# Conditioned attention on one Trainium2 core: the last two GpSimd operations moved to VectorE

## The chip, the core and the metric

The kernel runs on one core of a Trainium2 chip. A core has five engines that run their own instruction streams and meet only at semaphores: TensorE (PE, matrix products, its weight loads shown as PEld), VectorE (DVE), ScalarE (ACT), GpSimd (POOL) and SyncE (SP, which here only issues transfers). Sixteen DMA engines move data between the device memory and the on-chip memories, SBUF (128 partitions) and PSUM (128 partitions in 8 banks, where TensorE writes). The metric is the device time of one execution in microseconds (us).

## What is computed

The inputs are x, 8 batches of 512 rows of 512 features, one conditioning vector of 512 features for each batch, and the weights and biases of one attention layer with 16 heads of 32 features. All is in 32-bit floating point.

```python
Q = _split_heads(x @ Wq.T + bq)
K = _split_heads(x @ Wk.T + bk)
V = _split_heads(x @ Wv.T + bv)
tQ = _split_heads(tokens @ Wq.T + bq)
tK = _split_heads(tokens @ Wk.T + bk)
cQ = Q + tQ
cK = K + tK
scores = jnp.einsum('bhqd,bhkd->bhqk', cQ, cK) / jnp.sqrt(jnp.float32(HEAD_DIM))
attn = jax.nn.softmax(scores, axis=-1)
out = jnp.einsum('bhqk,bhkd->bhqd', attn, V)
...
x = x + _L0_cond_ref(x, cond_1024[:, None, :], ...)
```

So for each query row of each head: weights exp(score - maximum), their sum as the denominator, the weighted sum of the value rows divided by it, and x added.

## The kernel before

**Tiles.** A tile is one batch and a group of four heads (128 features), so there are T = 8 x 4 = 32 tiles, 0 to 31. A tile's scores are 4 heads of 512 x 512. TensorE makes the scores, VectorE takes row maxima, ScalarE exponentials, and TensorE multiplies the exponentials with the value rows (`times_v`). The main loop runs over tiles 1 to 28 and mixes the steps of neighbouring tiles; tiles 29, 30 and 31 are written out by hand behind it, and all that this change touches is in that last part, where `t = T - 1` (tile 31) and `t - 1` is tile 30.

**What sets the order.** The order on TensorE, ScalarE, VectorE and GpSimd is the order in which the program text issues the operations (`manual_schedule`). A framework adds the semaphores. An engine works through its queue in order, so an instruction that waits holds everything behind it. A transfer is issued by the queue that it names: `nc.sync` is SyncE's, `nc.scalar` ScalarE's.

**Tile 30's output.** For the earlier tiles, `send` (line 809) transposes the product with V on VectorE into the layout of the output (32 x 32 blocks), multiplies by the reciprocal denominators on GpSimd (line 813) and adds x there (line 814). Tile 29 goes that way (`send_parts`), and its line 814 is the last GpSimd operation ahead of the two that are moved. For tile 30 the same steps are written out: the denominators come from a product with ones of the summed exponentials (`times_ones(acc, pd, ...)`, line 755), are transposed (line 1267) and inverted (line 1270); the product with V is transposed into `y30` (line 1272); GpSimd multiplies `y30` by the reciprocals (line 1274) and adds `x30`, which is x with the bias of the values in it (line 1275). `store_30` (line 1277) sends one 32-partition quarter of `y30` at a time to the output: quarters 0 and 1 by SyncE (line 1282), 2 by ScalarE (line 1294), 3 by ScalarE as the very last transfer of the program (line 1325). All four are issued at line 1280.

**Tile 31's end.** While this happens TensorE makes tile 31's last exponentials' scores, denominators (line 755) and product with V (line 745). Then:

- VectorE multiplies the denominators with x into `part_x` (line 1291), and ScalarE copies the denominators (line 1293).
- In two halves VectorE adds `part_x` to the product with V (line 1302) and TensorE transposes the sum back (line 1304). Between the halves TensorE transposes the copied denominators (`untranspose`, line 836).
- VectorE inverts the denominators (line 1309) and multiplies each half by them (line 1314), so that (product + denominator x x) / denominator = attention + x.
- Four stores follow (line 1321), two each by ScalarE and SyncE, and quarter 3 of tile 30.

At the end of the program (line 1352 in the profile) each engine drains and then all engines meet.

Of the kernel before, what the change touches and what calls it, by code (L numbers as in the profile page):

```python
# [12 lines left out]
ALU = mybir.AluOpType  # L13
# [4 lines left out]
def kernel(  # L18
# [38 lines left out]
    nc = tc.nc  # L57
    P = 128
# [93 lines left out]
    BL = 32  # L152
    NB = S // BL

    def spread(a, d, n=1):

        return a.rearrange("(f j) d -> j f d", j=BL)[:, :, d : d + n * BL]
# [557 lines left out]
    def exponentials(t, kc, at=None):  # L715

        bank = [bank_of(i) for i in at] if at else [banks(i) for i in range(HG)]
        for j in range(HG):
            r = slice(j * HD, j * HD + 3)
            nc.tensor.matmul(bank[j], onesb[r, :], maxT[t][r, :], start=True, stop=False)  # L720
        for j in range(HG):
            r = slice(j * HD, (j + 1) * HD)
            nc.tensor.matmul(  # L723
                bank[j],
                qkT["k", t][r, kc * P : (kc + 1) * P],
                qkT["q", t][r, :],
                start=False,
                stop=True,
            )
        for pr in range(NP):  # L730
            e = room_for_e(t, kc, pr)
            es[t, kc, pr] = e
            for i in range(2):
                nc.scalar.activation(e[:, i, :], bank[pr * 2 + i], AF.Exp)  # L734
# [99 lines left out]
    def untranspose(o, pt):  # L834
        for qc in range(NS):
            nc.tensor.transpose(  # L836
                pt[:, qc * P : (qc + 1) * P], o[:, qc * P : (qc + 1) * P], ident
            )
# [136 lines left out]
    def late_part(i):  # L975
        return late[0][:, i, :]
# [292 lines left out]
    rec = op.tile([P, NB, 1], F32, tag="recs", name=f"recs_{t - 1}")  # L1269
    nc.vector.reciprocal(rec, den[:, :, 0:1])  # L1270
    y30 = late_part(13).rearrange("p (f e) -> p f e", e=BL)
    nc.vector.transpose(y30.rearrange("p f e -> p (f e)"), parts[t - 1])
    x30 = xr.pop(t - 1)
    nc.gpsimd.tensor_tensor(y30, y30, rec.broadcast_to([P, NB, BL]), ALU.mult)
    nc.gpsimd.tensor_tensor(y30, y30, x30, ALU.add)

    def store_30(queue, hs):
        b, g = divmod(t - 1, G)
        for h in hs:
            queue.dma_start(spread(out[b], h * P + g * BL), y30[h * BL : (h + 1) * BL])  # L1280

    store_30(nc.sync, (0, 1))
    exponentials(t, 3, (4, 2, 0, 1))
    times_v(t, 2, pv)
    pd = bank(7)
# [5 lines left out]
    nc.vector.tensor_tensor(part_x, pd, xr[t], ALU.mult)  # L1291
    den = late_part(11)
    nc.scalar.copy(den, pd)
    store_30(nc.scalar, (2,))
    oT = late[0][:, 0, :]
    y = late[0][:, 1, :].rearrange("p (c s) -> p c s", c=NS)
    rec = op.tile([P, NS, HG, 1], F32, tag="rec", name="rec")
# [3 lines left out]
    for i in range(2):  # L1301
        nc.vector.tensor_tensor(oT[:, two[i]], pv[:, two[i]], part_x[:, two[i]], ALU.add)  # L1302
        for qc in (i * 2, i * 2 + 1):
            nc.tensor.transpose(  # L1304
                po[i][:, qc * P : (qc + 1) * P], oT[:, qc * P : (qc + 1) * P], ident
            )
        if i == 0:
            untranspose(den, pi)
    nc.vector.reciprocal(  # L1309
        rec, pi.rearrange("p (c h e) -> p c h e", c=NS, h=HG)[:, :, :, 0:1]  # L1310
    )
# [45 lines left out]
```

## Time and profile before

| | |
|---|---|
| median of 3 runs | 681.99 us (680.9 to 684.14) |
| profiled execution, whole | 682.65 us |
| profiled execution, span | 680.4 us |
| TensorE busy | 660.6 us (97%) |
| VectorE busy | 578.9 us (85%) |
| ScalarE busy | 544.6 us (80%) |
| GpSimd busy | 340.7 us (50%) |

The profile is of one execution, so its own time and span stand beside the median. A row of a group of instructions reads: line, engine, operation, what it writes <- what it reads, shapes, count | busy us, mean ns of one | idle time of the engine before them and what ended it. A row of the timeline reads: start, duration, engine, line, operation, and in brackets the engine's idle time before it and what released it; neighbours of one kind are merged, so that "x2" is two instructions from the first one's start to the last one's end. An engine's name with q (POOLq, SPq) means its sequencer: drains, semaphores and the issue of transfers, which don't count as busy.

### The profile page before, as it was taken

To read this page: it belongs to the slowest core of one execution; us is meant where nothing else is said; L and a number is where in the kernel's file an instruction comes from. 1 tells how busy PE (TensorE), PEld (TensorE's weight loads), DVE (VectorE), ACT (ScalarE), POOL (GpSimd) and SP (SyncE) were. 2 spreads that over 40 slices of the span, in tenths; PEclk is the share of its full clock that TensorE was granted. 3 is DMA by queue.
4 is the path that set the end of the run, shared out by engine and by line. 5 is a ranking of instruction groups with operands and counts; after the bars stand their busy time and mean duration, and the time that the engine had idled before them with its cause. 6 is when DMAs were issued, how large, how long until landed. Compare 5 with 4: busy or idle time off the path is not lost. (4 is left out here: it accounts for less than half of the span.)

```text
span 680.4 us, 22874 instructions
## 1 busy us (share of the span) xinstructions
PE 660.6 (97%) x9100; PEld 312.6 (46%) x9100; DVE 578.9 (85%) x821; ACT 544.6 (80%) x1397; POOL 340.7 (50%) x449
## 2 busy tenths in 40 slices
PE   7989999999999999999999999999999999999993
PEld 6444454544544444444544444454544544454421
DVE  5897988989899898979889897898989898897793
ACT  1568788988979898898889888788988989897771
POOL 5551563565446464466635664464644666352531
PEclk9999999999999999999999999999999999999997
DMA  9718439386574938658383865729376573822011
GB/s 203 129 29 206 126 68 224 69 200 152 128 190 85 223 79 209 142 133 208 71 223 70 211 139 134 188 67 237 80 201 151 132 178 66 220 47 56 16 18 32
DMA packets 140814, 90.85 MB, mean 134 GB/s; under 512 B 117436, under 2 KB 126308, under 8 KB 140708
## 3 DMA queue, kind: packets, MB, share of 16 engines
q1 hardware_dynamic: 132196, 73.78, 47.5%
q0 software_dynamic: 5568, 14.95, 8.7%
q8 instruction: 72, 1.18, 0.8%
q10 hardware_dynamic: 2944, 0.66, 0.5%
q14 instruction: 34, 0.28, 0.1%
HBM read 20.27 MB, written 8.39 MB: 42 GB/s over the span
## 5 line engine op out<-in xcount | busy, mean ns | idle before, releaser
L664 ACT ACTIVATE psum<-psum,nmax 128x512 f32<-128x512 f32 x256 | 169.0, 663 | 52.5 <-DVE nmax L584 40.1
L584 DVE TENSOR_REDUCE nmax<-psum 128x1 f32<-128x512 f32 x270 | 171.4, 680 | 46.0 <-PE psum L617 45.5
L734 ACT ACTIVATE arena<-psum 128x512 f32<-128x512 f32 x264 | 136.9, 602 | 33.8 <-PE psum L723 24.4
L617 PE MATMUL psum<-kT,qT 32*128 32x512 f32 x1024 | 157.5, 621 | 1.4 <-ACT psum L664 1.4
L664 ACT ACTIVATE arena<-psum,nmax 128x512 f32<-128x512 f32 x224 | 152.6, 697 | 5.3 <-issue 4.2
L626 DVE TENSOR_REDUCE nmax<-psum 128x2 f32<-128x1024 f32 x115 | 139.3, 1212 | 1.1 <-PE psum L617 1.1
L637 DVE STREAM_TRANSPOSE blocks<-blocks 128x1024 f32<-128x1024 f32 x112 | 132.2, 1218 | 0.3 <-DMA blocks<-arena 0.2
L648 POOL DMA_DIRECT2D blocks<-arena x112 | 56.1, 506 | 78.8 <-ACT arena L664 69.2
L813 POOL TENSOR_TENSOR res<-res,recs 128x512 f32<-128x512 f32 x30 | 31.5, 1049 | 120.9 <-DVE res L812 120.9
L617 PEld LDWEIGHTS psum<-kT,qT 32*128 32x128 f32 x1024 | 59.5, 182 | 64.9 <-issue 24.0
L745 PE MATMUL psum<-arena,v 128*32 128x512 f32 x576 | 69.4, 597 | 0.0
L723 PE MATMUL psum<-qT,kT 32*128 32x512 f32 x528 | 68.5, 589 | 0.0
L745 PE MATMUL psum<-blocks,v 128*32 128x256 f32 x896 | 52.1, 381 | 0.0
L459 PE MATMUL psum<-wc_v,xc 128*32 128x256 f32 x768 | 50.6, 381 | 1.4 <-ACT v L497 1.4
L664 ACT ACTIVATION_READ_ACCUMULATOR psum<-psum,nmax 128x1 f32 x256 | 51.9, 203 | 0.0
L664 ACT ACTIVATION_READ_ACCUMULATOR arena<-psum,nmax 128x1 f32 x224 | 47.8, 213 | 0.0
L459 PE MATMUL psum<-xc,wc_q 128*32 128x256 f32 x720 | 47.4, 381 | 0.0
L459 PE MATMUL psum<-xc,wc_k 128*32 128x256 f32 x720 | 47.4, 381 | 0.0
L812 DVE STREAM_TRANSPOSE res<-psum 128x512 f32<-128x512 f32 x28 | 20.1, 717 | 23.3 <-PE psum L745 23.3
L814 POOL TENSOR_TENSOR xr<-res,xr 128x512 f32<-128x512 f32 x30 | 38.5, 1282 | 2.4
L207 POOL TENSOR_TENSOR xr<-xr,wT_q 128x512 f32<-128x512 f32 x30 | 38.4, 1279 | 0.2
L745 PEld LDWEIGHTS psum<-blocks,v 128*32 128x32 f32 x896 | 26.4, 110 | 25.0 <-ACT arena L734 10.6
(184 smaller groups left out, 934.4 us busy)
## 6 DMA issues: line engine op xcount, KB each, us to landing
blocks<-arena SPq DMA_DIRECT2D x336, 128.0 KB, 3.8
blocks<-arena POOLq DMA_DIRECT2D x112, 128.0 KB, 3.9
xr<-in_x_dram SPq DMA_DIRECT2D x60, 128.0 KB, 2.6
x<-in_x_dram SPq DMA_DIRECT2D x56, 128.0 KB, 3.5
out_dram<-xr SPq DMA_DIRECT2D x56, 128.0 KB, 2.4
w_q<-in_L_cond_Wq_dram SPq DMA_DIRECT2D x4, 256.0 KB, 4.4
w_k<-in_L_cond_Wk_dram SPq DMA_DIRECT2D x4, 256.0 KB
w_v<-in_L_cond_Wv_dram SPq DMA_DIRECT2D x4, 256.0 KB, 8.3
```

Of the source, the lines that this page charges most:

```text
L207: nc.gpsimd.tensor_tensor(xr[t], xr[t], bias, ALU.add)
L459: nc.tensor.matmul(pt[r], still[:, r], moving, start=(kc == kcs[0]), stop=(kc == kcs[-1]))
L584: nc.vector.tensor_reduce(nmax[t][:, qc, j : j + 1, 0], pt, AX.X, ALU.max, negate=True)
L617: nc.tensor.matmul(pt, qkT["q", t][r, qc * P : (qc + 1) * P], qkT["k", t][r, :], start=True, stop=True,)
L626: nc.vector.tensor_reduce(nmax[t][:, qc, pr * 2 : pr * 2 + 2, 0], pt, AX.X, ALU.max, negate=True)
L637: nc.vector.transpose(e, e)
L648: queue.dma_start(to.rearrange("p c h s -> p (c h s)"), of)
L664: nc.scalar.activation(to, of, AF.Exp, bias=nmax[t][:, qc, j, :], accum_out=sums[t][:, qc, j, :],)
L723: nc.tensor.matmul(bank[j], qkT["k", t][r, kc * P : (kc + 1) * P], qkT["q", t][r, :], start=False, stop=True,)
L734: nc.scalar.activation(e[:, i, :], bank[pr * 2 + i], AF.Exp)
L745: nc.tensor.matmul(pt[j * HD : (j + 1) * HD, at], vs[b % 2][:, kc, (g * HG + j) * HD : (g * HG + j + 1) * HD], e, start=(kc == chunks[0]), ...
L814: nc.gpsimd.tensor_tensor(xr[t], y, xr[t], ALU.add)
```

## The change

The multiplication and the addition that make tile 30's output are issued on VectorE instead of GpSimd. The multiplication keeps its place in the text, behind the transpose of line 1272. The addition moves down, behind both halves of tile 31's additions (line 1302) and ahead of its reciprocal (line 1309). The stores of quarters 0, 1 and 2 move with it, and are issued behind the addition; quarter 3 stays the last transfer. GpSimd has no operation behind tile 29's line 814.

```diff
     x30 = xr.pop(t - 1)
-    nc.gpsimd.tensor_tensor(y30, y30, rec.broadcast_to([P, NB, BL]), ALU.mult)
-    nc.gpsimd.tensor_tensor(y30, y30, x30, ALU.add)
+    nc.vector.tensor_tensor(y30, y30, rec.broadcast_to([P, NB, BL]), ALU.mult)
 
     def store_30(queue, hs):
...
-    store_30(nc.sync, (0, 1))
     exponentials(t, 3, (4, 2, 0, 1))
     times_v(t, 2, pv)
     pd = bank(7)
...
     den = late_part(11)
     nc.scalar.copy(den, pd)
-    store_30(nc.scalar, (2,))
...
         if i == 0:
             untranspose(den, pi)
+    nc.vector.tensor_tensor(y30, y30, x30, ALU.add)
+    store_30(nc.sync, (0, 1))
+    store_30(nc.scalar, (2,))
     nc.vector.reciprocal(
```

## The prediction

> **What bounds the kernel now.** I began with the end of the chain of waits, because the edit touches only the last stage. Columns: start, duration (both us), what.
>
> ```profile
> 667.89 0.88 PE psum L745 x6
> 668.77 0.02 issue
> 668.80 0.43 DVE late L1302
> ...
> 669.72 0.45 PE psum L836 x4
> 670.17 0.02 issue
> 670.19 0.27 DVE rec L1309
> ...
> 670.70 0.61 DVEq L1352
> ```
>
> The chain ends at 671.3, and the page's span is 680.4: 9.1 us of the program hold no compute on it. So the second view is the rows of line 1352, where the program ends (`q` marks an engine's sequencer; min/median/max duration in ns, then first and last start), first whole and then for 674.82 to 679.6 alone:
>
> ```profile
> span 680.4 us, 22874 instructions
> L1352 POOLq DRAIN  x3: 46/102/11037, 668.6 to 680.1; - x3
> L1352 SPq DRAIN  x3: 7/7/7, 674.8 to 679.9; - x3
> L1352 ACTq DRAIN  x2: 8/79/150, 673.1 to 679.9; - x2
> ```
>
> ```profile
> L1352 POOLq DRAIN  x1: 11037/11037/11037, 668.6 to 668.6; - x1
> L1352 SPq DRAIN  x1: 7/7/7, 674.8 to 674.8; - x1
> ```
>
> Each engine drains, and then all meet. ScalarE has drained at 673.2, SyncE (which waits for the stores) at 674.8. GpSimd's drain starts at 668.6 and takes 11.04 us, to 679.6, and in the 4.8 us before its end nothing else is recorded. From 679.6 to the span's end are 0.8 us of meeting. The waits of SyncE and the transfers of 676 to 681 agree:
>
> ```profile
> SPq L1352 <- PEq L1352: 5.5, 2, 5.0
> DMA packets 0, 0.00 MB, mean 0 GB/s; under 512 B 0, under 2 KB 0, under 8 KB 0
> ```
>
> The releaser named there is only the last engine to be let go; what ends at 679.6 is GpSimd's drain. So **the end is set by GpSimd**, not by tile 31's arithmetic. Is that length owed to the last GpSimd work? The start of the program has the only other drain of GpSimd outside the meeting, and it follows four tiny fills:
>
> ```profile
> L1343 POOLq DRAIN  x1: 183/183/183, 0.3 to 0.3; - x1
> ```
>
> A drain is thus not 11 us by nature; this one lasts until 9.7 us after GpSimd's last operation (table below: 668.62 + 1.27 = 669.89). One instance can't say what those 9.7 us are counted from. I read them as GpSimd's own, counted from its last work, because the drain starts as soon as its sequencer is through, while no other engine has finished.
>
> The stage itself, in order of time:
>
> ```profile
> 651.96 1.27 POOL L814 TENSOR_TENSOR xr<-res,xr 128x512 f32<-128x512 f32 x1
> 667.49 1.05 POOL L1274 TENSOR_TENSOR late<-late,recs 128x512 f32<-128x512 f32 x1 [14.26 <-DVE late L1272]
> ```
>
> ```profile
> 666.76 0.65 DVE L1272 STREAM_TRANSPOSE late<-parts 128x512 f32<-128x512 f32 x1
> ...
> 667.97 0.69 DVE L1291 TENSOR_TENSOR late<-psum,xT 128x512 f32<-128x512 f32 x1 [0.55 <-PE psum L755]
> 668.62 1.27 POOL L1275 TENSOR_TENSOR late<-late 128x512 f32<-128x512 f32 x1
> 668.69 0.59 ACT L1293 COPY late<-psum 128x512 f32<-128x512 f32 x1 [2.42 <-DVE late L1291]
> 668.80 0.76 DVE L1302 TENSOR_TENSOR late<-psum,late 128x256 f32<-128x256 f32 x2
> ...
> 669.55 0.60 PE L836 MATMUL psum<-ident,late 128*128 128x128 f32 x4
> ...
> 669.92 0.85 SPq L1280 DMA_DIRECT2D out_dram<-late  x2
> 669.92 0.38 ACTq L1280 DMA_DIRECT2D out_dram<-late  x1
> ...
> 670.19 0.26 DVE L1309 RECIPROCAL rec<-psum 128x16 f32<-128x16 f32 x1 [0.63 <-PE psum L836]
> 670.55 0.76 DVE L1314 TENSOR_TENSOR late<-psum,rec 128x256 f32<-128x256 f32 x2
> 671.00 1.60 SPq L1321 DMA_DIRECT2D out_dram<-late  x2
> 671.01 1.32 ACTq L1321 DMA_DIRECT2D out_dram<-late  x2
> 672.37 0.65 ACTq L1280 DMA_DIRECT2D out_dram<-late  x1
> ```
>
> **The change, part by part.** *Removed from GpSimd*: 1.05 us (L1274) and 1.27 us (L1275). Its last operation becomes L814, which ends at 653.23, as nothing of GpSimd lies between. The drain then starts at about 652 and ends at 653.23 + 9.7 = 662.9. What hides it is the work of tile 31 and its stores, to 674.8: a cover of 11.9 us. Without that cover it would cost 4.8 us, as now. The end is next set by SyncE: 674.8 + 0.8 = 675.6, so the ceiling of the gain is 680.4 - 675.6 = **4.8 us**, before what VectorE's new work takes off.
>
> *Added to VectorE*: two elementwise operations on 128x512 with both operands in SBUF. The nearest rows:
>
> ```profile
> L386 DVE TENSOR_TENSOR xc<-xc,xT 128x512 f32<-128x512 f32 x1 | 0.7, 692 | 0.1
> L1302 DVE TENSOR_TENSOR late<-psum,late 128x256 f32<-128x256 f32 x2 | 0.8, 420 | 0.1
> L1314 DVE TENSOR_TENSOR late<-psum,rec 128x256 f32<-128x256 f32 x2 | 0.8, 420 | 0.1
> ```
>
> So 0.69 us each; the broadcast factor costs nothing (420 ns at L1314, with one, and at L1302, without).
>
> *The multiplication* follows the transpose L1272, which ends at 667.41, and runs to about 668.13. It fills the 0.55 us in which VectorE waited for TensorE, and L1291 starts 0.08 to 0.17 us late. (Independent neighbours overlap by 0.08 us: the L1302 pair takes 0.76 us, not 2 x 0.42.) L1291 then ends at 668.74 to 668.82. Two wait for it. L1302 waits also for the product with V, which ends at 668.77, and so comes 0.0 to 0.1 us late; I take 0.06. ScalarE's copy of the denominators would end near 669.4, and the transposes that read it start at 669.55: covered, by some 0.15 us, and beyond that it would delay L1309.
>
> *The addition* stands between L1302, which ends at 669.56, and the reciprocal L1309. There VectorE waited 0.63 us for L836; the addition takes 0.69, less 0.08 of overlap at one side. That is 0 to 0.06 us more. Its operands are old by then (the multiplication, and x with its bias), so it waits for nothing; queued behind it are L1309, the pair L1314 and through them the four stores of L1321. Together I take **0.1 us** late at L1314. The ends for these two steps are 0 (both fit the gaps) and 1.38 us (neither does, 2 x 0.69).
>
> *Moved stores*: three of tile 30's four are released by the addition near 670.25 instead of by GpSimd at 669.89, some 0.35 us later. On SyncE the two take 0.85 us, to 671.1, which puts its part of L1321 back by 0.1 to 0.15 us, to an end near 672.75. On ScalarE one takes 0.38 us and is through by 670.7, before L1314 has anything ready. ScalarE's last store (672.37 + 0.65 = 673.02 now) stays the last issue, and moves by the 0.1. In the transfers of 671.3 to 673 (tenths busy of the DMA engines, slices of 0.0425 us) there is a hole from about 671.9 to 672.3:
>
> ```profile
> DMA  9999999999987631000000016999999999999996
> ```
>
> Before the hole are tile 30's three stores, behind it the other five. A delay of 0.35 us slides the three into the hole of 0.4 and pushes nothing; if it were 0.2 longer, the last landing would move by 0.1 to 0.2.
>
> *Sum*: -4.8 + 0.1 = -4.7 us: span 675.7. The profiled execution took 682.65 us, 2.25 more than its span, and would be 677.95; it stands 0.66 above the median of the runs, 681.99, against which the forecast is **677.3 us** (-0.69%).
>
> **Rivals.**
>
> *The drain belongs to the program's end, not to GpSimd's work.* Then it ends some 4.8 us behind the last landing whoever works last, and only the 0.1 us stays: 682.1. For it: one instance, and a long drain was seen only at the end. Against it: it starts at 668.6, 6 us before SyncE is through, and GpSimd's later drains in the meeting take 46 and 102 ns. [...]
>
> *Slower: the early drain holds up VectorE.* While GpSimd worked on L814, a VectorE cast took six times that of its like, and ended with it at 653.28:
>
> ```profile
> 652.07 1.21 DVE L678 CAST split<-nmax 128x16 bf16<-128x16 f32 x1
> ...
> 653.54 0.20 DVE L680 CAST split<-rest 128x16 bf16<-128x16 f32 x1
> ...
> 654.91 1.22 DVE L1147 TENSOR_TENSOR acc<-arena 128x1024 f32<-128x1024 f32 x1
> ```
>
> If the drain did the same, it would lie from 653.2 to 662.9 beside tile 30's and 31's sums, which read SBUF twice and keep VectorE without a gap (stretch, its length, then busy us of PE, PEld, DVE: 6.00 of 6.00):
>
> ```profile
> 660.00:666.00 6.00, 5.98 (x55) 1.47 (x51) 6.00 (x7) 4.84 (x11) 0.00 (x0) 1.00 0.00 0
> ```
>
> The sums would start 8.0 us late; the 0.55 of idle before L1291 gives some back, and -4.7 + 8.0 - 0.5 = +2.8: 684.8. It decides from a hold of about 5.2 us on. Against it: after 669.9 the present drain ran beside L1309 and L1314, which took their usual 0.26 and 0.42 us. [...]
>
> *Both operations in the open.* If the semaphores between them and their neighbours cost enough that neither fits its gap, 1.4 us of the 4.8 are given back: 678.6.
>
> **How the numbers follow.** Forecast 0.80, drain of the end 0.12, both in the open 0.05, held VectorE 0.03. For the range: gains from 4.8 (nothing late) down to 3.4 (both in the open), each against the runs of before, 680.9 to 684.14: 676.1 to 680.7. It leaves out the two rivals at 682.1 and 684.8, 0.15 together, and takes 0.1 more below. No change is what lies within 0.5%, 3.4 us here, about what a measurement of this kernel can tell apart: the forecast is beyond it with 0.92, the exposed case with half, the other two lie within or a little above. Faster 0.77, same 0.19, slower 0.04.
>
> **What would show it.** Right: GpSimd's long drain starts near 652 and ends before 665; SyncE's second drain stands at 674.9 to 675.1 and the span ends 0.8 behind it; L1309 starts at 670.2 to 670.35; tile 30's stores are issued at 670.2 to 670.35. Wrong: the long drain still ends some 5 us after SyncE's (first rival); L1147 and L1149 behind 654 last longer than 1.22 us or start late (second); L1314 starts after 671.5 (third).

## The result and the profile after

| | before | after |
|---|---|---|
| median of 9 runs | 682.41 us (680.7 to 684.14) | 677.85 us (675.44 to 680.18) |
| ratio, after to before | | 0.9941 (95%: 0.9922 to 0.9959) |
| profiled execution: span | 680.4 us | 676.1 us |
| start of L1267 to the end of the span | 14.57 us | 9.93 us |

The kernel is faster by 0.6% (0.4 to 0.8%). The forecast was 677.3 us. The last row of the table is the sharper measure: L1267 is VectorE's transpose of tile 30's denominators, among the last steps that both kernels share ahead of the change. What lies ahead of it differs by some tenths of a microsecond and more from execution to execution (it starts at 665.85 in the profile of before and at 666.13 in that of after); what lies behind it took 4.64 us less.

The rows of line 1352, where the program ends, in the changed kernel, first whole, then for 652 to 653 alone (min/median/max in ns, first and last start):

```profile
L1352 POOLq DRAIN  x3: 46/102/11028, 652.2 to 675.8; - x3
L1352 SPq DRAIN  x3: 7/7/7, 675.2 to 675.5; - x3
L1352 ACTq DRAIN  x2: 8/79/150, 673.4 to 675.5; - x2
```

```profile
L1352 POOLq DRAIN  x1: 11028/11028/11028, 652.2 to 652.2; - x1
```

GpSimd's drain is as long as before, 11.03 us against 11.04, but starts at 652.2 and ends at 663.2, beside tile 30's and 31's work. GpSimd's last operation, from its timeline:

```profile
652.25 1.26 POOL L814 TENSOR_TENSOR xr<-res,xr 128x512 f32<-128x512 f32 x1
```

It ends at 653.51, and the drain 9.73 us later: to the hundredth the distance of before (679.62 less 669.89). The waits of SyncE's queue show what took its place at the end:

```profile
SPq L1352 <- DMA out_dram<-late: 1.7, 3, 0.7
SPq L1352 <- PEq L1352: 0.7, 2, 0.5
```

The wait for the other engines, 5.5 us before, is 0.7; what SyncE waits for is now the landing of the stores, and 0.77 us behind its second drain the span ends. VectorE and the issues of the stores, from the timelines of the changed kernel:

```profile
667.04 0.65 DVE L1272 STREAM_TRANSPOSE late<-parts 128x512 f32<-128x512 f32 x1
667.73 0.69 DVE L1274 TENSOR_TENSOR late<-late,recs 128x512 f32<-128x512 f32 x1
668.34 0.68 DVE L1289 TENSOR_TENSOR late<-psum,xT 128x512 f32<-128x512 f32 x1
669.13 0.75 DVE L1299 TENSOR_TENSOR late<-psum,late 128x256 f32<-128x256 f32 x2
669.80 0.68 DVE L1306 TENSOR_TENSOR late<-late 128x512 f32<-128x512 f32 x1
670.52 0.26 DVE L1309 RECIPROCAL rec<-psum 128x16 f32<-128x16 f32 x1
670.88 0.76 DVE L1314 TENSOR_TENSOR late<-psum,rec 128x256 f32<-128x256 f32 x2
```

```profile
670.51 0.85 SPq L1279 DMA_DIRECT2D out_dram<-late  x2
671.46 1.49 SPq L1321 DMA_DIRECT2D out_dram<-late  x2
```

```profile
670.51 0.38 ACTq L1279 DMA_DIRECT2D out_dram<-late  x1
671.34 1.32 ACTq L1321 DMA_DIRECT2D out_dram<-late  x2
672.70 0.65 ACTq L1279 DMA_DIRECT2D out_dram<-late  x1
```

(L1289, L1299 and L1306 are the lines 1291, 1302 and the moved addition; L1279 is 1280 of before.) VectorE has no hole longer than 0.11 us from L1272 to L1314. Less the 0.28 us by which L1267 itself stands later, L1289 starts 0.09 us late, L1309 and L1314 0.04.

### The profile page after: what moved, and what is told of

Read it like the earlier page. It is cut to its first block, busy times and chain, and to the rows that moved or that the text cites. A ratio compares the mean times of both kernels' runs of the same rounds, so it can differ in the third digit from the quotient of the medians.

```text
span 676.1 us, 22875 instructions
## 1 busy us (share of the span) xinstructions
PE 661.0 (98%) x9100; PEld 313.7 (46%) x9100; DVE 579.0 (86%) x823; ACT 544.1 (80%) x1397; POOL 337.7 (50%) x447
## 4 chain that ended last, share of the span: by engine, by line
PE 91%; DVE 3%; DMA 2%; SPq 1%; issue 1%; ACT 1%; POOL 0%; DVEq 0%; ACTq 0%
PE psum L459 41%; PE psum L617 19%; PE psum L745 16%; PE psum L723 7%; PE psum L720 3%; PE psum L402 2%; DMA blocks<-arena 1%; SPq L648 1%; DMA early<-in_L_cond_Wk_dram 1%; DVE acc L1149 1%; PE psum L1175 1%; DVE nmax L626 1%; PE psum L852 0%; DVE acc L1147 0%; DVE nmax L584 0%
## 5 line engine op out<-in xcount | busy, mean ns | idle before, releaser
L814 POOL TENSOR_TENSOR xr<-res,xr 128x512 f32<-128x512 f32 x30 | 38.4, 1280 | 2.4
L745 PEld LDWEIGHTS psum<-blocks,v 128*32 128x32 f32 x896 | 26.4, 110 | 25.0 <-ACT arena L734 10.6
```

Of the source, the lines that this page charges most:

```text
L745: nc.tensor.matmul(pt[j * HD : (j + 1) * HD, at], vs[b % 2][:, kc, (g * HG + j) * HD : (g * HG + j + 1) * HD], e, start=(kc == chunks[0]), ...
L814: nc.gpsimd.tensor_tensor(xr[t], y, xr[t], ALU.add)
```

## The experiments

All are compared by the time from the start of L1267 to the end of the span, and by the ends of the two drains that can set it. Columns: by how much GpSimd's long drain outlasts GpSimd's last operation, its end and that of SyncE's second drain, both from L1267, then the time from L1267 to the end. Each row is one profiled execution; L1267 stands for the same transpose in every kernel, though its line number shifts by 2 or 3 where lines were added ahead of it.

| kernel | drain outlasts by | GpSimd's drain ends | SyncE's drain ends | L1267 to end |
|---|---|---|---|---|
| before | 9.73 | 13.78 | 8.99 | 14.57 |
| after | 9.73 | -2.89 | 9.16 | 9.93 |
| multiplication alone moved | 9.73 | 13.37 | 9.03 | 14.17 |
| after + small late operation | 9.73 | 11.02 | 9.17 | 11.81 |
| after + small early operation | 9.73 | 4.19 | 9.17 | 9.94 |
| after + long late operation | 9.73 | 12.71 | 10.40 | 13.50 |
| after, addition early | 9.73 | -2.88 | 9.78 | 10.76 |
| after, quarter 3 first | 9.73 | -2.89 | 9.10 | 9.87 |
| after without the two operations | 9.73 | -2.89 | 9.01 | 9.78 |
| before, no software transfer | 0.07 | 4.11 | 9.13 | 9.83 |
| before, one software transfer | 0.16 | 4.21 | 9.19 | 9.95 |
| before, 70 software transfers | 5.81 | 9.86 | 9.01 | 10.65 |
| after, 230 software transfers | 9.00 | -3.63 | 9.17 | 9.94 |

In all rows but one the end lies 0.69 to 0.79 us behind the later of the two drains; in the row with the early addition it is 0.98. The measure repeats closely: the changed kernel and two variants of it whose end is alike (small early operation, 230 transfers) give 9.93, 9.94 and 9.94. The long late operation and the four kernels on software transfers were executed once each, so of them only this stage and the drain's length are compared.

**The multiplication alone.**

```diff
-    nc.gpsimd.tensor_tensor(y30, y30, rec.broadcast_to([P, NB, BL]), ALU.mult)
+    nc.vector.tensor_tensor(y30, y30, rec.broadcast_to([P, NB, BL]), ALU.mult)
     nc.gpsimd.tensor_tensor(y30, y30, x30, ALU.add)
```

> One part of the change alone: the multiplication goes to VectorE, the addition and its stores stay with GpSimd where they were. Measured from the start of the denominators' transpose (L1267) to the span's end: 14.56 us before, 9.92 us after. Theory (GpSimd's long drain lasts until 9.73 us after the end of its last operation, and 0.79 us of meeting follow): the addition can start at about 668.2 instead of 668.62 on the time axis of before, so all but 0.4 us of the gain is missing: 14.1 us, about 682.0 us in all. Rival (the gain is GpSimd's work itself, taken off in two halves): half the gain, 12.2 us, about 680 us.

Measured: 14.17 us, 681.64 us in all, ratio to before 0.9993 (0.9975 to 1.001). GpSimd's last operation and its drain:

```profile
668.06 1.27 POOL L1275 TENSOR_TENSOR late<-late 128x512 f32<-128x512 f32 x1 [14.99 <-DVE late L1274]
```

```profile
L1352 POOLq DRAIN  x1: 11038/11038/11038, 668.0 to 668.0; - x1
```

Nearly half of GpSimd's work behind tile 29 is gone (1.05 of 2.32 us), but under a tenth of the gain is there: 0.40 us, by which the addition now ends earlier. What counted was when GpSimd stopped, not how much it did.

**A small operation, late.** Added to the changed kernel behind `x30 = xr.pop(t - 1)`:

```diff
+    nc.gpsimd.tensor_tensor(
+        late_part(14)[:, :NB].unsqueeze(2), rec, rec, ALU.add
+    )
```

> The changed kernel with one small GpSimd operation added (128x16, adds tile 30's reciprocals to themselves into an unused place), which can start when VectorE's reciprocal L1270 is done, 1.1 us behind the start of L1267. Nothing reads its result. Theory, drain counted from the end of GpSimd's last operation: 1.1 + 0.3 + 9.73 + 0.79 = 11.9 us from L1267 to the end, 2.0 us of the gain given back by an operation of 0.3 us; about 679.8 us. Rival, drain counted from the start of the last operation (11.03 us): 1.1 + 11.03 + 0.79 = 12.9 us, about 680.8 us. Rival, the gain comes from something else than when GpSimd stops: 9.9 us, 677.9 us.

Measured: 11.81 us from L1267 to the end.

```profile
666.05 0.21 POOL L1274 TENSOR_TENSOR late<-recs 128x16 f32<-128x16 f32 x1 [13.70 <-DVE recs L1270]
```

```profile
L1355 POOLq DRAIN  x1: 9982/9982/9982, 666.0 to 666.0; - x1
```

An operation of 0.21 us, whose result nobody reads and which delays no other engine, gives back 1.88 us of the 4.64. The drain is shorter than that of the changed kernel by what the operation is shorter (9.98 against 11.03, 0.21 against 1.26 us): it is counted from the operation's end, where the rival had 12.9 us. The runs in all say less: 678.76 us, ratio 0.9946 (0.9923 to 0.9968), an interval that overlaps the changed kernel's. The time ahead of L1267 varies by as much as is looked for (it starts at 664.97 in this profile, at 666.13 in the changed kernel's).

**A small operation, early.**

```diff
     nc.vector.tensor_tensor(parts[t - 1], pa, parts[t - 1], ALU.add)
+    nc.gpsimd.tensor_tensor(
+        late_part(14)[:, :NB], parts[t - 1][:, :NB], parts[t - 1][:, :NB], ALU.add
+    )
```

> The same small GpSimd operation, but on tile 30's partial output, ready some 6.7 us ahead of L1267 (659.4 in the changed kernel's profile). Theory: the drain ends 9.73 us behind it, near 669.4, and SyncE's second drain at 675.3 covers it: 9.9 us from L1267 to the end, 677.9 us, no change. Rival (any further GpSimd work behind tile 29 costs): 0.3 us or more slower.

Measured: 9.94 us, 677.44 us in all, ratio 0.9932 (0.991 to 0.9954). The drain ends 4.19 us behind L1267 and SyncE's, at 9.17, covers it: the operation cost nothing at this place (9.94 us against 9.93). The operation itself took its time (GpSimd's timeline, then VectorE's):

```profile
658.84 1.13 POOL L1255 TENSOR_TENSOR late<-parts 128x16 f32<-128x16 f32 x1 [5.97 <-DVE parts L1254]
```

```profile
658.68 2.37 DVE L1149 TENSOR_TENSOR acc<-acc,arena 128x1024 f32<-128x1024 f32 x2
```

1.13 us for what took 0.21 in the run before, beside a sum of VectorE that reads SBUF twice and ends near 659.9.

**A long operation, late.** The same place as the small late one:

```diff
+    nc.gpsimd.tensor_tensor(
+        late[0][:, 14:16, :].rearrange("p a (b e) -> p (a b) e", e=2 * BL),
+        acc[0].rearrange("p a (b e) -> p (a b) e", e=2 * BL),
+        rec.broadcast_to([P, NB, 2 * BL]),
+        ALU.mult,
+    )
```

> As the small late operation, but 128x1024 long (tile 30's summed exponentials times the reciprocals, into an unused place), 2.1 to 2.4 us. It tells the two ways of counting apart. From the end of the operation: 1.1 + 2.2 + 9.73 + 0.79 = 13.8 us from L1267 to the end. From its start, or a length that grows with nothing: 12.9 us, as with the small one by that rival. A side reading: VectorE's multiplication L1274, which reads SBUF twice, falls beside it; if the two engines lock each other out as with the cast L678 (1.21 us beside GpSimd's L814), it ends with the GpSimd operation plus its own 0.69 us, else it takes 0.69 us.

Measured: 13.50 us. The operation took 1.90 us, less than the 2.1 to 2.4 expected. The count from its end then gives 1.07 + 1.90 + 9.73 + 0.79 = 13.5; the count from its start (12.9) falls.

```profile
667.97 1.90 POOL L1274 TENSOR_TENSOR late<-acc,recs 128x1024 f32<-128x1024 f32 x1 [13.69 <-DVE recs L1270]
```

```profile
668.50 1.92 DVE L1280 TENSOR_TENSOR late<-late,recs 128x512 f32<-128x512 f32 x1
670.35 0.68 DVE L1295 TENSOR_TENSOR late<-psum,xT 128x512 f32<-128x512 f32 x1
```

VectorE's multiplication took 1.92 us in place of 0.69 and ended 0.55 behind GpSimd's operation: it was held up beside it, as the cast L678 was in the profile of before (1.21 us, where its like L680 took 0.20), though it needed 0.14 less behind it than the whole operation that was expected. In the run before it was GpSimd's operation that was held (1.13 us for 0.21). L1295 starts 0.48 us behind the end of GpSimd's operation and took its usual 0.68.

**The place of the addition.**

```diff
     nc.vector.tensor_tensor(y30, y30, rec.broadcast_to([P, NB, BL]), ALU.mult)
...
+    nc.vector.tensor_tensor(y30, y30, x30, ALU.add)
+    store_30(nc.sync, (0, 1))
     exponentials(t, 3, (4, 2, 0, 1))
...
     nc.scalar.copy(den, pd)
+    store_30(nc.scalar, (2,))
...
-    nc.vector.tensor_tensor(y30, y30, x30, ALU.add)
-    store_30(nc.sync, (0, 1))
-    store_30(nc.scalar, (2,))
```

> Place of the addition: it stands right behind the multiplication on VectorE, with its stores, instead of behind tile 31's additions. Theory: it falls ahead of L1289 (part_x), which is on the path, and pushes it by about 0.6 us; tile 30's stores start 1.3 us earlier and win nothing: 10.4 us from L1267 to the end (9.92 in the changed kernel), about 678.3 us. Rival: the transfers at the end are the bound, and earlier stores give the 0.6 us back: 9.9 us.

Measured: 10.76 us, 0.83 more than the changed kernel.

```profile
667.04 0.69 DVE L1274 TENSOR_TENSOR late<-late,recs 128x512 f32<-128x512 f32 x1
667.77 0.69 DVE L1281 TENSOR_TENSOR late<-late 128x512 f32<-128x512 f32 x1
668.38 0.68 DVE L1291 TENSOR_TENSOR late<-psum,xT 128x512 f32<-128x512 f32 x1
...
670.56 0.26 DVE L1309 RECIPROCAL rec<-psum 128x16 f32<-128x16 f32 x1 [0.64 <-PE psum L836]
```

The addition needs the multiplication's result and starts only behind its end (667.73, 667.77), so L1291 comes 0.73 us later than L1289 does in the changed kernel, and the hole of 0.64 us ahead of L1309 stands empty again. L1314 starts 0.74 us later and SyncE finds the last transfer landed 0.74 us later, so the earlier stores give nothing back. SyncE's drain ends only 0.62 us later, because of the order of its waits (see *The landing* below). 0.2 more lie in the meeting of the engines, in VectorE's last drain (VectorE's drains of this run, then of the changed kernel; the last start and the shortest are those of the meeting):

```profile
L1352 DVEq DRAIN  x2: 137/400/664, 671.1 to 675.8; - x2
L1352 DVEq DRAIN  x2: 19/339/659, 671.0 to 675.6; - x2
```

SyncE's second drain had ended at 675.21 here and at 675.29 there. Why VectorE's came late is open, and no other run shows it. The price of the wrong place is thus about what a whole operation lasts, more than the 0.6 us that was expected. The difference is too small for the times in all (678.25 us, ratio 0.9933, 0.9906 to 0.996).

**Quarter 3 first.**

```diff
-    store_30(nc.scalar, (2,))
+    store_30(nc.scalar, (2, 3))
...
-    store_30(nc.scalar, (3,))
```

> A version that may beat both: quarter 3 of tile 30 is stored by ScalarE right behind quarter 2, not as the last transfer of the program. Theory: with the drain out of the way SyncE's last landing is the bound; ScalarE's last issue (0.65 us, 672.70 to 673.36) falls away, the last issue is then SyncE's at 672.95, and the landing comes 0.3 us earlier: 9.6 us from L1267 to the end, about 677.5 us. Rival: the DMA engines are full from 672.4 on, and the bytes count, not the issue: 9.9 us.

Measured: 9.87 us against 9.93; in all 679.0 us, ratio 0.9943 (0.9921 to 0.9965). ScalarE's issues:

```profile
670.80 0.93 ACTq L1279 DMA_DIRECT2D out_dram<-late  x2
671.82 1.55 ACTq L1321 DMA_DIRECT2D out_dram<-late  x2
```

The last issue ends 6.96 us behind L1267 in place of 7.23, but SyncE's drain comes only 0.06 earlier. The expected 0.3 us were wrong. SyncE's wait for the transfer that landed last ends 8.93 us behind L1267 in both kernels, and the 0.06 is one wait less behind it (see *The landing* below). So the last issue isn't what the end waits for; that the transfers' bytes are the limit fits, and isn't shown by this run alone. As a version that beats both kernels it doesn't count: 0.06 us can't be measured in the times.

**Without the two operations.**

```diff
-    nc.vector.tensor_tensor(y30, y30, rec.broadcast_to([P, NB, BL]), ALU.mult)
...
-    nc.vector.tensor_tensor(y30, y30, x30, ALU.add)
```

> Tile 30's multiplication and addition are left out (its output is stored undivided and without x), all else as in the changed kernel; the difference is what VectorE's two operations cost in their gaps. Theory: 0.05 us at L1314 and up to 0.35 us in the start of tile 30's stores, which slide into a hole of the transfers: 9.75 us from L1267 to the end, about 677.7 us. Rival: both in the open, 1.4 us: 8.5 us, 676.4 us.

Measured: 9.78 us. VectorE's two operations, 1.37 us long together, cost 0.15 us where the change put them. Only 0.04 of that is delay on VectorE: L1314 starts 4.75 us behind L1267 in the changed kernel, and its like (L1312) 4.71 us behind it here, where L1267 starts at 666.19.

```profile
670.90 0.76 DVE L1312 TENSOR_TENSOR late<-psum,rec 128x256 f32<-128x256 f32 x2
```

The rest is two waits of SyncE, 0.06 us each (see *The landing* below).

**No software transfers.** A transfer that GpSimd's queue issues is listed by the profile as software_dynamic (q0); the kernel before has 118 of them (112 exchanges, 4 first weights, 2 biases). In this run, which is otherwise the kernel before, SyncE issues them all:

```diff
-    BY_POOL = (3,)
+    BY_POOL = ()
...
-        nc.gpsimd.dma_start(
+        nc.sync.dma_start(
             cond_sp[B + i :: BL, :P], bias.rearrange("(h c) -> h c", h=HG)
...
-    load_first("k", Wk, [nc.gpsimd] * HG)
+    load_first("k", Wk, [nc.sync] * HG)
```

> What are the 9.73 us? The kernel before, with every transfer that GpSimd's queue issued (the 112 block exchanges, the first weights and biases) issued by SyncE instead; GpSimd's operations are as before. Theory A (the drain's length belongs to software transfers): GpSimd's last drain is under 1 us behind its last operation, and the span ends 0.8 us behind SyncE's second drain, 9.8 us from L1267 to the end. Theory B (it belongs to any end of GpSimd's work): 9.73 us as before, 14.6 us from L1267 to the end. The main loop may become slower, since SyncE's queue then carries all exchanges; only the end is compared.

Measured: 9.83 us from L1267 to the end, with both operations still on GpSimd, and the drain's length is gone:

```profile
683.27 1.27 POOL L1275 TENSOR_TENSOR late<-late 128x512 f32<-128x512 f32 x1
```

```profile
L1352 POOLq DRAIN  x1: 1371/1371/1371, 683.2 to 683.2; - x1
```

The drain ends 0.07 us behind the addition. So the 9.73 us aren't owed to GpSimd's arithmetic but to the software transfers of the whole program, the last of which was long done (in the kernel before its packets have ended by 588.7 us, 80 us ahead of the drain). As a remedy it is no use: L1267 starts at 680.5 in place of 665.8, and the whole takes 692.11 us. SyncE now issues all exchanges, and its queue holds 17% of this kernel's chain of waits (shares of the span by engine; the chain of before reaches back over the last 2% only, so the two can't be set side by side):

```profile
PE 55%; SPq 17%; DMA 11%; DVE 8%; POOL 3%; ACT 3%; issue 2%; DVEq 0%; ACTq 0%
```

**One, 70 and 230 software transfers.** One: as in the run before, but the biases of the queries go by GpSimd again. 70: in the kernel before, the exchanges stay with GpSimd for tiles under 16 only. 230: in the changed kernel each exchange is cut in two.

```diff
+        (nc.gpsimd, nc.sync)[i].dma_start(
...
+                queue = nc.gpsimd if a in BY_POOL and t < T // 2 else nc.sync
...
+                for r in (slice(0, 16), slice(16, BL)) if a in BY_POOL else (slice(0, BL),):
+                    queue.dma_start(to[r], of[r])
```

> As the kernel without software transfers, but one single transfer (the biases of the queries, at the program's start) is issued by GpSimd's queue again. It tells what the 9.73 us count. Theory (any use of software transfers brings the whole length): GpSimd's drain ends 9.73 us behind its last operation, 14.6 us from L1267 to the end. Rival (the length grows with the transfers, 118 in the kernel before): 9.73 / 118 = 0.08 us for one, so under 0.3 us behind the last operation, 9.8 us to the end. Rival (it belongs to the block exchanges from SBUF to SBUF): also under 0.3 us.

> The kernel before, with GpSimd's block exchanges kept for tiles under 16 and given to SyncE for the others: 64 + 6 = 70 software transfers instead of 118. Two points are known, 0.07 us behind the last operation with none and 9.73 with 118; one transfer gave 0.16. Theory (the drain's length grows with their number): 0.07 + 70 x 9.66 / 118 = 5.8 us behind the last operation; the addition ends 4.05 us behind L1267, so the drain ends at 9.85 and the span at 10.6 us behind L1267. Rival (it has the full length from some number on): 9.73 us, 14.6 us to the end. Rival (only what was issued late counts): none in the second half, under 0.3 us, 9.8 us to the end.

> The changed kernel with each of GpSimd's 112 block exchanges cut into two transfers of 16 partitions: 224 + 6 = 230 software transfers of the same bytes. The drain lies under tile 31's work, so only its own length is read. If it grows with the number of transfers (0.082 us each from 0, 70 and 118): 0.07 + 230 x 0.082 = 18.9 us behind GpSimd's last operation, to about 672.4, still covered by SyncE's drain at 675.3. If with their packets, which need not double (5568 now, at 1.73 ns): under 18 us, in proportion to the packets that the profile counts. If with the bytes: 9.73 us as now. The main loop may become slower, as GpSimd issues twice as often.

Measured, GpSimd's drains with one, 70 and 230 transfers:

```profile
L1352 POOLq DRAIN  x1: 1468/1468/1468, 685.4 to 685.4; - x1
```

```profile
L1352 POOLq DRAIN  x1: 7122/7122/7122, 674.6 to 674.6; - x1
```

```profile
L1354 POOLq DRAIN  x1: 10298/10298/10298, 665.3 to 665.3; - x1
```

The profile counts the software transfers' packets and MB, here with 70 transfers, with the 118 of the kernel before, and with 230:

```profile
q0 software_dynamic: 3264, 8.66, 5.1%
q0 software_dynamic: 5568, 14.95, 8.7%
q0 software_dynamic: 7360, 14.96, 10.7%
```

The drain outlasts the last operation (1.27 us in each) by 0.16, 5.81 and 9.00 us. With none, one, 70 and 118 transfers it lies on a straight line in their number: 0.07 + 70 x 0.082 = 5.8, and 0.07 + 118 x 0.082 = 9.7. (Lines through the packets or the bytes come near it at 70, with 5.73 and 5.67, and are a little worse.) With 70 transfers the kernel's end came 10.65 us behind L1267, as the line says (10.6). The step to 230 breaks it: neither the count of transfers (18.9) nor that of packets (12.8 at 1.73 ns each) nor the bytes (9.73) gives 9.00, although none of the three is smaller than with 118. Whether the length stops growing from some number on, or a half-sized transfer adds less than half of what a whole one does, wasn't tested; what the drain goes through stays open. None of these kernels is faster in all either: they took 694.4 us with one transfer, 684.39 with 70 and 690.97 with 230, where the kernel before took 684.38, 682.17 and 681.39 beside them.

## Why the prediction was right, point by point

- *The end is set by GpSimd's drain, counted from its last operation.* Right, and shown: the drain moved with the last operation in nine kernels with the same transfers, always ending 9.73 us behind its end, and the small late operation brought 1.88 us of the end back alone. The reading was made from one instance; the profile of after by itself removed the first rival, since the drain ends 12 us ahead of SyncE's second drain.
- *Its length is GpSimd's own.* Right as far as it went. That it is owed to the software transfers was not foreseen. That the 9.73 us could be carried over unchanged was therefore in part luck: the change left all 118 transfers in place, which the prediction didn't know to matter. The short drain at the program's start (183 ns, from 0.3 us on), which I quoted against a fixed length, fits that: GpSimd's queue issues its first transfer only at 1.5 us.
- *Ceiling 4.8 us, then SyncE is the bound.* Right: SyncE's second drain ends at 675.29 and the span at 676.06. I had 674.9 to 675.1, on an axis on which L1267 stood 0.28 us earlier; less that, it ends at 675.0.
- *The two operations.* 0.69 and 0.68 us against 0.69. L1289 0.09 us late (0.08 to 0.17 stated), L1299 0.04 (0.06 taken), L1314 0.04 where I took 0.1: the addition fits its hole with its overlap.
- *The stores.* Tile 30's three came 0.31 us later (0.35), SyncE's part of L1321 0.17 later (0.1 to 0.15). The transfers of 671.7 to 673.4 in the changed kernel (tenths busy, slices of 0.0425 us as in the prediction):

```profile
DMA  8999999999999998764200489999999999999779
```

The hole of about 0.4 us has shrunk to about 0.2: the three stores slid into it, as I had it, and the last landing came 0.05 us later, about as much as VectorE's 0.04.

- *The landing.* SyncE's drain moved by 0.17 us where the sum had 0.1, from a part that I hadn't seen. At its end SyncE waits for its transfers' semaphores one after the other, in rows of 28 ns. Of before, for 674.6 to 674.8, and of after, for 674.6 to 675.25:

```profile
L1352 SPq EVENT_SEMAPHORE  x1: 28/28/28, 674.7 to 674.7; - x1
L1352 SPq DRAIN  x1: 7/7/7, 674.8 to 674.8; - x1
```

```profile
L1352 SPq EVENT_SEMAPHORE  x3: 28/28/28, 675.0 to 675.2; - x3
L1352 SPq DRAIN  x1: 7/7/7, 675.2 to 675.2; - x1
```

Before, the wait for the transfer that landed last stood last. After, two that had landed already stood behind it and cost 0.06 us each; with the 0.05 by which the last landing itself came later that makes up the 0.17.

- *Sum.* -4.64 us from L1267 to the end against -4.7; 4.56 by the medians, 4.0 (2.8 to 5.3) by the ratio. The median of before had been 681.99 us over three runs and is 682.41 over nine, which is most of why 677.85 stands above the forecast of 677.3. By the prediction's own terms the chance of a faster kernel is 0.80 x 0.92 + 0.05 x 0.5 = 0.76, where it has 0.77.
- *Rivals.* Drain at the program's end: fell. Held VectorE: fell for the drain, beside which the sums L1147 and L1149 kept their 1.21 to 1.23 us; between operations such a hold was measured, 1.92 us for 0.69 beside the long late operation, and it matters for where GpSimd work is put. Both operations in the open: fell by the run without them, 0.15 us against 1.4.

VectorE operations with one input in PSUM kept their times beside GpSimd's in the profile of before: L1291 took 0.69 us beside L1274 and the pair L1302 0.76 beside L1275, against 0.68 and 0.75 in the changed kernel, where GpSimd has no operation there. Whether the place of the inputs decides was not tested.

## What to carry to other kernels

Look at what ends last behind the last result: here the chain of waits ended with compute 9.1 us short of the span, and the drains of the engines told which one held the meeting. Where GpSimd issues transfers, see where its last operation ends and whether its drain (here 9.73 us beyond that operation with 118 transfers) lies under other work: an operation of 0.21 us late in the stage brought the end from 9.93 to 11.81 us behind L1267, and one that ended 5.5 us ahead of L1267 cost nothing (9.94). What is taken over by another engine goes into holes of its timeline: 1.37 us of VectorE delayed its last operations by 0.04 us and the end by 0.15 in the two holes, and the operations by 0.74 more when one of the holes was missed.

## What the runs showed of the hardware

GpSimd's drain at the end of the program differed with the transfers that its queue had issued over the whole program: it ended 0.07 us behind GpSimd's last operation with none, 0.16 with one, 5.81 with 70 and 9.73 with 118, but 9.00 with 230, of which 224 were half-sized. In the kernel before the last of them had landed 80 us ahead of the drain. In all nine kernels with the same 118 transfers the drain outlasted the last operation by 9.73 us, whether that operation took 0.21 us or 1.90, and whether GpSimd had stood idle ahead of it (14.26 us ahead of the last two operations in the kernel before) or had worked without a gap (the changed kernel).

VectorE and GpSimd met not only at semaphores. Beside an operation of the other, VectorE's multiplication took 1.92 us for 0.69, its cast L678 1.21 where its like took 0.20, and GpSimd's small early operation 1.13 for 0.21; beside GpSimd's drain VectorE's sums kept their 1.21 to 1.23.
